# A fused attention and feed-forward block on one core: the first batch taken tile by tile, and the last product split into three pieces

## The chip, the core and the metric

The kernel runs on one core of a Trainium2 chip. The core has five engines that work side by side, each with its own queue of instructions taken in order: PE (TensorE, matrix products into PSUM), DVE (VectorE), ACT (ScalarE), POOL (GpSimd) and SP (SyncE, which here only issues DMA transfers). They wait for each other through semaphores. The metric is the time of one launch in device microseconds (us). Times are of one core, so the slowest core is this one.

## What is computed

Eight batches of 1024 rows with 256 columns, all in float32. Each row is normalized (`xn`), goes through an attention without softmax and through a feed-forward layer, and both results are added to the row:

```python
xn = layernorm(x)                                  # x: (8, 1024, 256)
qkv = xn @ qkv_w + qkv_b                           # 16 heads of 16 columns
q, k = l2norm(q), l2norm(k)
kv = einsum('bhnd,bhne->bhde', k, v)
attn = einsum('bhnd,bhde->bhne', q, kv) @ proj_w + proj_b
ffn = relu(xn @ W1 + b1) @ W2 + b2                 # 256 -> 1024 -> 256
out = x + attn + ffn
```

## The kernel before

**Tiling.** A batch is eight tiles of 128 rows, numbered 0 to 7. Tiles 0 to 3 are its first half, 4 to 7 its second. Products need the rows as columns, so `xn` is turned into `xnT`. For the first batch this is done on PE (`turn_on_pe`, L279: a turn of a 128x128 block is a PE operation against an identity, four to a PSUM bank, and a 128x512 copy by ACT or DVE takes the bank to `xnT`). For later batches DVE and DMA do it while other work runs. The hidden layer, the later projections and the output product are formed by a seven-product scheme over 2x2 blocks: sums of blocks (`sums_of_x`, `sums_of_w1`, `s3_of_x` and their like, on POOL) replace the eighth product.

**Order.** The schedule is manual: each engine runs its instructions in the order in which the program text issues them. An instruction that has to wait holds up everything behind it on its own engine. PSUM tiles named by `bank` (L90) rotate through seven buffers, so a new one waits until the tile seven places back has been read.

**The start.** `load` (L96) issues the loads of `x` on SP: L128 brings the first half of batch 0 in two pieces of two tiles, L129 the query and key weights, L130 the second half in two pieces, L131 the bias of query and key (`qkvb_sb`, spread to all partitions). Then come `b1`, `w1` and the value weights. At L874 PE runs 20 turns of the identity (`WARM`). `norm_stats` (L241) forms mean and variance on DVE and the square root on ACT; `norm_scale` (L255) takes the reciprocal; `norm_apply` (L264) scales a tile on DVE (L275) or on ACT (L271). L877 to L888 do this for tiles 0 to 3, turn them, and then for tiles 4 to 7.

**The projection of batch 0.** `project` (L313) takes tile after tile: two products into one bank (L330, `kc` 0 and 1), the addition of the bias on DVE (L334), the squares on ACT (L336), and their sums on DVE (L339), delayed by one tile. `between` runs a function behind a given tile: `second_half` (L892), behind tile 2, turns tiles 4 to 7 and the rows of `b1` and issues the block sums of x. Behind the projection come L901 to L903 (a block sum, the load of batch 1 into the same `x` buffer, the remaining weights), and then the loop over batches, which begins with `hidden` (L635 is its product).

**The end.** `second` (L764) forms the output product. For the last batch, the second half's output is turned back on PE (`back_on_pe`, L807: turns at L813, addition to `x` at L818) instead of by DVE and POOL. Its last block has two pieces of 256 columns in two banks (`ds`, `parts`, L824 and L825): both products are issued (L860), then both sums on DVE (L862), then for each piece the turn, the addition and a store on SP (L867). The first half's rows go out by four stores (`store(0)`, L803), also on SP.

The lines on which the two ends turn:

```python
load(0, (0,), 2)
load_wqkv(of_qk)
load(0, (1,), 2)
load_qkvb(of_qk)
```

Of the kernel before, what the change touches and what calls it, by code (L numbers as in the profile page):

```python
# [9 lines left out]
F32 = mybir.dt.float32  # L10
AF = mybir.ActivationFunctionType
# [5 lines left out]
def kernel(  # L17
# [46 lines left out]
    S = 32  # L64
    R = P // S
    NP, HP = NT // 2, HT // 2
    WARM = 20
    LN_EPS = 1e-5
    L2_EPS = 1e-12

# [10 lines left out]
    def rows_v(v, b, n):  # L81

        return v[b].rearrange("(n p t) c -> n p t c", n=2, p=P)[n]
# [6 lines left out]
    def bank(shape, name):  # L90

        return psum.tile(shape, F32, tag="bank", name=name)

    xs, xqs, xns, xnTs, xSs, hTs, qks, qTs, mixes, Ms, hSs = ({} for _ in range(11))

    def load(b, halves=(0, 1), pieces=1):  # L96

        if b not in xs:
            xs[b] = one.tile([P, NT, C], F32, tag="x", name=f"x_{b}")
        gt = HT // pieces  # L100
        for n in halves:
            for g in range(pieces):
                nc.sync.dma_start(
                    out=xs[b][:, n * HT + g * gt : n * HT + (g + 1) * gt, :],
                    in_=rows_v(x, b, n)[:, ts(g, gt), :],
                )

    def load_squares(b, halves=(0, 1)):
        xqs[b] = one.tile([P, 2, R, HT, CJ], F32, tag="xq", name=f"xq_{b}")
# [15 lines left out]
        nc.sync.dma_start(out=qkvb_sb[:, cols], in_=qkv_b[cols].partition_broadcast(P))  # L125

    of_qk, of_v = slice(0, 2 * C), slice(2 * C, 3 * C)
    load(0, (0,), 2)  # L128
    load_wqkv(of_qk)  # L129
    load(0, (1,), 2)  # L130
    load_qkvb(of_qk)  # L131
    b1_rows = one.tile([FC, P], F32, tag="gT", name="b1_rows")
    nc.sync.dma_start(out=b1_rows, in_=b1.rearrange("(k p) -> k p", p=P))
# [107 lines left out]
    def norm_stats(b, tiles):  # L241

        xt, n = xs[b], len(tiles)
        st = work.tile([P, NT, 6], F32, tag="st", name=f"st_{b}_{tiles[0]}")[:, :n, :]
        mv = small.tile([P, NT, 2], F32, tag="mv", name=f"mv_{b}_{tiles[0]}")[:, :n, :]
        for i, t in enumerate(tiles):
            nc.vector.bn_stats(st[:, i, :], xt[:, t, :])
        for i in range(n):
            nc.vector.bn_aggr(mv[:, i, :], st[:, i, :])
        rstd = small.tile([P, NT], F32, tag="rstd", name=f"rstd_{b}_{tiles[0]}")[:, :n]  # L250
        nc.scalar.activation(rstd, mv[:, :, 1], AF.Sqrt, bias=eps_sb)
        for i, t in enumerate(tiles):
            stats[b, t] = i, mv, rstd

    def norm_scale(b, tiles, on_act):  # L255
        i, mv, rstd = stats[b, tiles[0]]
        nc.vector.reciprocal(rstd, rstd)
        if on_act:
            nmr = small.tile([P, NT], F32, tag="nmr", name=f"nmr_{b}_{i}")[:, : len(tiles)]
            nc.vector.scalar_tensor_tensor(nmr, mv[:, :, 0], -1.0, rstd, ALU.mult, ALU.mult)  # L260
            for t in tiles:
                stats[b, t] += (nmr,)

    def norm_apply(b, tiles):  # L264
        if b not in xns:
            xns[b] = one.tile([P, NT, C], F32, tag="xn", name=f"xn_{b}")
        for t in tiles:
            xt, xn = xs[b][:, t, :], xns[b][:, t, :]
            i, mv, rstd, *nmr = stats.pop((b, t))
            if nmr:  # L270
                nc.scalar.activation(  # L271
                    xn, xt, AF.Identity, bias=nmr[0][:, i : i + 1], scale=rstd[:, i : i + 1]
                )
            else:
                nc.vector.tensor_scalar(  # L275
                    xn, xt, mv[:, i, 0:1], rstd[:, i : i + 1], ALU.subtract, ALU.mult
                )
# [32 lines left out]
            turns["x", b] = turn(xnTs[b], xns[b], f"x_{b}")  # L310
        next(turns["x", b])

    def project(b, between={}, with_norms=True):  # L313


        xnT = xnTs[b]
        if b not in qks:
            qks[b] = one.tile([P, NT, 2 * C], F32, tag="qk", name=f"qk_{b}")
        qk = qks[b]
        late = []  # L320
        for h in range(2):
            ss = small.tile([P, HT, 2 * H], F32, tag="ssk" if h else "ssq", name=f"ss_{b}_{h}", bufs=1)
            all_ss[b, h] = ss
            for s in range(2):
                norms_of[b, h, s] = ss[:, :, ts(s, H)]
            for i in range(HT):
                t = h * HT + i
                pq = bank([P, 512], f"pq_{b}_{t}")
                for kc in range(KC):
                    nc.tensor.matmul(  # L330
                        pq, xnT[:, kc, t // 2, :, t % 2], wqkv_sb[:, kc, 0 : 2 * C],
                        start=(kc == 0), stop=(kc == KC - 1),
                    )
                nc.vector.tensor_tensor(qk[:, t, :], pq, qkvb_sb[:, 0 : 2 * C], ALU.add)  # L334
                sq = work.tile([P, 2 * C], F32, tag="yt", name=f"sq_{b}_{t}")
                nc.scalar.activation(sq, qk[:, t, :], AF.Square)  # L336
                while late:
                    late.pop(0)()
                late.append(lambda ss=ss, sq=sq, i=i: nc.vector.tensor_reduce(  # L339
                    ss[:, i, :], sq.rearrange("p (g d) -> p g d", d=D), AX.X, ALU.add  # L340
                ))
                if i == HT - 1 and with_norms:
                    late.append(lambda h=h, ss=ss: norms(b, h, ss))
                between.get(t, lambda: None)()
        while late:
            late.pop(0)()

# [408 lines left out]
    def product(dst, lhs, rhs, start, stop):  # L756

        for n, (l, r) in enumerate(zip(lhs, rhs)):
            nc.tensor.matmul(  # L759
                dst, l, r, start=start and n == 0, stop=stop and n == len(lhs) - 1,  # L760
                skip_group_check=True,
            )

    def second(b, early=lambda: None, between=lambda: None):  # L764
# [17 lines left out]
        def add(dst, p, q):  # L782
            nc.vector.tensor_tensor(dst, p, q, ALU.add)
            return dst
# [19 lines left out]
            for j in range(R):  # L804
                nc.sync.dma_start(out=squares_v(out, b, n, j), in_=xq[ts(j, S), n])

        def back_on_pe(m, y, us, name):  # L807


            tp = bank([P, HP, 2, R, S], f"tp{name}_{b}")  # L810
            for u in us:
                for w in range(2):
                    nc.tensor.transpose(  # L813
                        tp[:, u, w].rearrange("p j c -> p (j c)"), y[:, u, :, w], ident
                    )
            xh = xs[b].rearrange("p (n u w) (j m c) -> n m p (u w) j c", n=2, w=2, m=2, c=S)[1, m]
            at = slice(2 * us[0], 2 * us[-1] + 2)
            nc.vector.tensor_tensor(  # L818
                xh[:, at], xh[:, at], tp.rearrange("p u w j c -> p (u w) j c")[:, at], ALU.add
            )  # L820

        a, c_, d, e = (bank([P, HP, P, 2], f"po{s}_{b}") for s in "acde")

        ds = [d] if b < B - 1 else [d[:, 0], bank([P, HP, P, 2], f"pof_{b}")[:, 1]]  # L824
        parts = [slice(0, HP)] if b < B - 1 else range(HP)  # L825
        product(a, b11, a11, True, False)
        u1 = tmp("u1")
        nc.scalar.copy(u1, a)
# [1 line left out]
        u2 = add(tmp("u2"), c_, u1)  # L830
        early()
        u3 = tmp("u3")
        for du, u in zip(ds, parts):
            product(du, t3, [r[:, u] for r in s3], True, False)
            add(u3[:, u], du, u2[:, u])
        between()

        product(e, t1, s1, True, False)
# [13 lines left out]
        if b < B - 1:  # L852
            product(d, t4, a22, False, True)
            join(1, 0, d, u2)
            store(1)
        else:
            back_on_pe(1, y22, range(HP), "o22")
            y21 = tmp("y")
            for u in range(HP):
                product(ds[u], t4, [r[:, u] for r in a22], False, True)  # L860
            for u in range(HP):
                nc.vector.scalar_tensor_tensor(  # L862
                    y21[:, u], ds[u], ob[:, 2, 0:1], u2[:, u], ALU.add, ALU.add
                )
            for u in range(HP):
                back_on_pe(0, y21, (u,), f"o21_{u}")
                nc.sync.dma_start(  # L867
                    out=rows_v(out, b, 1)[:, ts(u, 2), :],
                    in_=xs[b][:, HT + 2 * u : HT + 2 * u + 2, :],
                )  # L870
        yield


    warm = bank([P, HT, P], "warm")  # L874
    for i in range(WARM):
        nc.tensor.transpose(warm[:, i % HT, :], ident, ident)
    norm_stats(0, range(0, 2))  # L877
    norm_stats(0, range(2, 4))
    xnTs[0] = big.tile([P, KC, NP, P, 2], F32, tag="xnT", name="xnT_0")
    for g in (0, 2):  # L880
        norm_scale(0, range(g, g + 2), False)
        norm_apply(0, range(g, g + 2))
    turn_on_pe(xnTs[0], xns[0], "x_0", (0,), (nc.scalar.copy, nc.vector.tensor_copy))
    for g in (4, 6):
        norm_stats(0, range(g, g + 2))
    for g in (4, 6):
        norm_scale(0, range(g, g + 2), True)
        norm_apply(0, range(g, g + 2))  # L888
    sums_of_w1()
    b1_sb = const.tile([P, FC], F32, tag="b1", name="b1_sb")  # L890

    def second_half():  # L892
        turn_on_pe(xnTs[0], xns[0], "x_0", (1,))
        b1_ps = bank([P, FC], "b1_ps")
        nc.tensor.transpose(b1_ps, b1_rows, ident[:FC, :FC])
        nc.vector.tensor_copy(b1_sb, b1_ps)
        sums_of_x(0, 0)
        sums_of_x(0, 1)

    project(0, {HT - 2: second_half}, False)  # L900
    s3_of_x(0)  # L901
    load(1)
    load_rest()  # L903
# [79 lines left out]
```

## Time and profile before

The median of three runs is 619.12 us (618.82 to 619.12). The profiled execution took 620.73 us, of which the span that the trace covers is 619.0 us.

| | busy us | share of the span |
|---|---|---|
| PE | 609.8 | 99% |
| POOL | 421.0 | 68% |
| DVE | 409.6 | 66% |
| PE weight loads | 346.1 | 56% |
| ACT | 210.1 | 34% |

| moment | us from the start of the span |
|---|---|
| first turn of the identity on PE | 1.36 |
| first tile pair of `x` landed, statistics begin | 3.46 |
| first turn of `xn` on PE | 6.27 |
| first product of the projection | 8.47 |
| first product of the hidden layer | 24.90 |
| last addition on DVE | 613.98 |
| end of the span | 619.0 |

The program has 6600 instructions and moves 43.3 MB by DMA, a mean of 70 GB/s. The mean granted clock of PE is 0.994 of full speed.

Reading: "busy" is the time in which an engine had an instruction running. A granted clock of 1.00 is PE's full speed. A row of the timeline gives the start, the duration, the engine, the line, the operation with what it writes and reads, the count, and in brackets how long the engine had been idle and what released it. The "chain that ended last" follows the program back from its last instruction, at each step to what released it.

### The profile page before, as it was taken

To read this page: it belongs to the slowest core of one execution; us is meant where nothing else is said; L and a number is where in the kernel's file an instruction comes from. 1 tells how busy PE (TensorE), PEld (TensorE's weight loads), DVE (VectorE), ACT (ScalarE), POOL (GpSimd) and SP (SyncE) were. 2 spreads that over 40 slices of the span, in tenths; PEclk is the share of its full clock that TensorE was granted. 3 is DMA by queue.
4 is the path that set the end of the run, shared out by engine and by line. 5 is a ranking of instruction groups with operands and counts; after the bars stand their busy time and mean duration, and the time that the engine had idled before them with its cause. 6 is when DMAs were issued, how large, how long until landed. Compare 5 with 4: busy or idle time off the path is not lost.

```text
span 619.0 us, 6600 instructions
## 1 busy us (share of the span) xinstructions
PE 609.8 (99%) x2011; PEld 346.1 (56%) x2011; DVE 409.6 (66%) x733; ACT 210.1 (34%) x355; POOL 421.0 (68%) x346
## 2 busy tenths in 40 slices
PE   8999999999999999999999999999999999999996
PEld 5465446457554666447564484644846457654454
DVE  5777754778748767577756876567865678527823
ACT  4355404352133513244142432425224352103500
POOL 2477997499916997279954799339992599914701
PEclk8999999999999999999999999999999999999998
DMA  7633101580026700275004820058101550004202
GB/s 237 131 66 97 40 0 31 123 176 13 0 52 141 147 2 1 71 167 103 0 1 111 172 58 1 15 123 172 33 0 35 128 110 1 0 7 97 69 1 68
DMA packets 139508, 43.32 MB, mean 70 GB/s; under 512 B 135880, under 2 KB 136272, under 8 KB 139472
## 3 DMA queue, kind: packets, MB, share of 16 engines
q1 hardware_dynamic: 139472, 42.89, 31.2%
q8 instruction: 16, 0.26, 0.2%
q14 instruction: 20, 0.16, 0.1%
HBM read 19.80 MB, written 8.39 MB: 46 GB/s over the span
## 4 chain that ended last, share of the span: by engine, by line
PE 96%; DVE 2%; DMA 1%; issue 0%; ACT 0%; SPq 0%; DVEq 0%; ACTq 0%
PE poa L759 11%; PE poe L759 11%; PE pod L759 10%; PE pha L635 8%; PE phe L635 8%; PE phd L635 8%; PE poc L759 6%; PE pq L330 5%; PE phc L635 4%; PE pqa L398 3%; PE pqe L398 3%; PE pqd L398 3%; PE gpe L565 2%; PE gpd L565 2%; PE gpa L565 2%; PE pqc L398 2%
## 5 line engine op out<-in xcount | busy, mean ns | idle before, releaser
L796 POOL TENSOR_TENSOR xq<-xq,yt_o 128x512 f32<-128x512 f32 x30 | 37.9, 1265 | 122.6 <-DVE yt_o L791 122.6
L642 ACT ACTIVATE hT<-hT,b_sb 128x512 f32<-128x512 f32 x96 | 68.9, 722 | 63.2 <-DVE hT L647 58.4
L190 POOL TENSOR_TENSOR hS<-hT 128x512 f32<-128x512 f32 x31 | 46.5, 1499 | 40.2 <-ACT hT L642 40.2
L635 PE MATMUL pha<-xnT,w_sb 128*128 128x512 f32 x128 | 65.4, 592 | 0.0
L759 PE MATMUL poa<-hT,w_sb 128*128 128x512 f32 x128 | 57.6, 592 | 0.0
L376 ACT ACTIVATE sq<-qk 128x512 f32<-128x512 f32 x48 | 28.9, 626 | 71.1 <-DVE qk L404 59.1
L647 DVE TENSOR_TENSOR hT<-phe,u 128x512 f32<-128x512 f32 x64 | 43.7, 684 | 6.7 <-PE phe L635 4.8
L192 POOL TENSOR_TENSOR hS<-hT,hS 128x512 f32<-128x512 f32 x31 | 39.6, 1276 | 2.4
L191 POOL TENSOR_TENSOR hS<-hS,hT 128x512 f32<-128x512 f32 x31 | 39.5, 1273 | 2.4
L791 DVE STREAM_TRANSPOSE yt_o<-y_o 128x512 f32<-128x512 f32 x30 | 33.0, 1099 | 11.4 <-ACT y_o L847 9.1
L194 POOL TENSOR_TENSOR hT<-hT 128x512 f32<-128x512 f32 x31 | 40.0, 1291 | 0.0
L759 PEld LDWEIGHTS poa<-hT,w_sb 128*128 128x128 f32 x128 | 23.8, 190 | 24.7 <-issue 24.2
L635 PEld LDWEIGHTS pha<-xnT,w_sb 128*128 128x128 f32 x128 | 23.8, 190 | 23.4 <-issue 22.2
L661 ACT COPY u<-pha 128x512 f32<-128x512 f32 x32 | 18.4, 575 | 51.6 <-PE pha L635 51.6
L647 DVE TENSOR_TENSOR u<-phc,u 128x512 f32<-128x512 f32 x32 | 21.8, 682 | 19.7 <-ACT u L661 10.6
L642 ACT ACTIVATE hT<-pha,b_sb 128x512 f32<-128x512 f32 x32 | 21.9, 683 | 33.2 <-PE pha L635 33.2
L635 PE MATMUL phe<-xS,w1t 128*128 128x512 f32 x64 | 32.7, 592 | 0.0
L635 PE MATMUL phe<-xS,w_sb 128*128 128x512 f32 x64 | 32.7, 592 | 0.0
L635 PE MATMUL phc<-xS,w1t 128*128 128x512 f32 x64 | 32.7, 592 | 0.0
L635 PE MATMUL phd<-xnT,w1t 128*128 128x512 f32 x64 | 32.7, 592 | 0.0
L635 PE MATMUL phd<-xnT,w_sb 128*128 128x512 f32 x64 | 32.7, 592 | 0.0
L271 ACT ACTIVATE xn<-x,nmr,rstd 128x256 f32<-128x256 f32 x56 | 28.4, 587 | 6.6 <-PE gpd L565 4.1
(191 smaller groups left out, 1311.5 us busy)
## 6 DMA issues: line engine op xcount, KB each, us to landing
xq<-in_L_attn_x_dram SPq DMA_DIRECT2D x60, 128.0 KB, 3.7
out_dram<-xq SPq DMA_DIRECT2D x60, 128.0 KB, 2.8
x<-in_L_attn_x_dram SPq DMA_DIRECT2D x14, 512.0 KB, 6.4
xnT<-turn_x SPq DMA_DIRECT2D x112, 64.0 KB, 2.1
qT<-turn_q SPq DMA_DIRECT2D x112, 64.0 KB, 2.2
x<-in_L_attn_x_dram SPq DMA_DIRECT2D x4, 256.0 KB, 4.0
w_sb<-in_L_ffn_W_dram SPq DMA_DIRECT2D x2, 512.0 KB, 7.8
w_sb<-in_L_ffn_W_dram SPq DMA_DIRECT2D x8, 128.0 KB, 3.2
```

The lines of the kernel that those rows point to most:

```text
L190: eng.tensor_tensor(s1, a21, a22, ALU.add)
L191: eng.tensor_tensor(s2, s1, a11, ALU.subtract)
L192: eng.tensor_tensor(s4, a12, s2, ALU.subtract)
L194: eng.tensor_tensor(a21, a11, a21, ALU.subtract)
L398: nc.tensor.matmul(dst[:, w, :], a[:, g, :, w], rhs, start=start and w == 0, stop=stop, skip_group_check=True,)
L565: nc.tensor.matmul(dst, l[:, t, :], r[:, t, :], start=start and t == 0, stop=stop and t == HT - 1, skip_group_check=True,)
L635: nc.tensor.matmul(dst, lhsT, rhs, start=start, stop=stop, skip_group_check=True)
L642: nc.scalar.activation(block(i, n, m), src, AF.Relu, bias=b1_sb[:, fc : fc + 1])
L647: nc.vector.tensor_tensor(dst, p, q, ALU.add)
L759: nc.tensor.matmul(dst, l, r, start=start and n == 0, stop=stop and n == len(lhs) - 1, skip_group_check=True,)
L791: nc.vector.transpose(yt.rearrange("p u w r c -> p u r w c"), y.rearrange("p u (s r) w -> p u r w s", r=R),)
L796: nc.gpsimd.tensor_tensor(xh, xh, yt.rearrange("p u w r c -> p (u w) r c"), ALU.add)
```

## The change

Start: 16 turns of the identity instead of 20. Tiles 0 and 1 are loaded singly, then the weights of query and key, then tiles 2 and 3, 4 and 5, 6 and 7 as pairs. Tiles 0 and 1 are each normalized by themselves, scaled on DVE and turned by a new `turn_tile`: two turns into one bank and one 128x256 copy on ACT. Tiles 2 and 3 are normalized before the projection begins and turned inside it, between the two products of tile 1. The same function then normalizes tiles 4 to 7 (4 and 5 scaled on ACT, 6 and 7 on DVE). These are turned between the two products of tile 3. The squares of tiles 0 to 2 are held until tile 3 has been projected.

End: the last batch's last block has three pieces, of 256, 128 and 128 columns, in three banks. The sum of a piece stands directly behind its product, and its turn behind the product of the next piece. Three stores instead of two: tiles 0 and 1 and then tile 2 of the second half are issued by ACT, tile 3 by SP.

```diff
-    WARM = 20
+    WARM = 16
...
-    load(0, (0,), 2)
+    load(0, (0, 1, 2))
     load_wqkv(of_qk)
-    load(0, (1,), 2)
+    load(0, (2, 4, 6, 8))
     load_qkvb(of_qk)
...
-    def project(b, between={}, with_norms=True):
+    def project(b, within={}, held_to=0, with_norms=True):
...
                 for kc in range(KC):
                     nc.tensor.matmul(
                         pq, xnT[:, kc, t // 2, :, t % 2], wqkv_sb[:, kc, 0 : 2 * C],
-                        start=(kc == 0), stop=(kc == KC - 1),
+                        start=(kc == 0), stop=(kc == KC - 1), skip_group_check=True,
                     )
+                    if kc == 0:
+                        within.get(t, lambda: None)()
                 nc.vector.tensor_tensor(qk[:, t, :], pq, qkvb_sb[:, 0 : 2 * C], ALU.add)
...
+                def square(t=t, ss=ss, i=i):
+                    sq = work.tile([P, 2 * C], F32, tag="yt", name=f"sq_{b}_{t}")
+                    nc.scalar.activation(sq, qk[:, t, :], AF.Square)
+                    return lambda: nc.vector.tensor_reduce(
+                        ss[:, i, :], sq.rearrange("p (g d) -> p g d", d=D), AX.X, ALU.add
+                    )
+
+                held.append(square)
+                while held and t >= held_to:
+                    late.append(held.pop(0)())
+                    while len(late) > 1:
+                        late.pop(0)()
...
-        def back_on_pe(m, y, us, name):
+        def back_on_pe(m, y, tiles, name):
...
-        ds = [d] if b < B - 1 else [d[:, 0], bank([P, HP, P, 2], f"pof_{b}")[:, 1]]
-        parts = [slice(0, HP)] if b < B - 1 else range(HP)
+        if b < B - 1:
+            parts = [lambda r: r]
+        else:
+            parts = [lambda r: r[:, 0], lambda r: r[:, 1, :, 0], lambda r: r[:, 1, :, 1]]
+        ds = [parts[0](d)] + [
+            part(bank([P, HP, P, 2], f"po{s}_{b}")) for s, part in zip("fg", parts[1:])
+        ]
...
+            for k in range(len(ds) + 1):
+                if k < len(ds):
+                    part = parts[k]
+                    product(ds[k], t4, [part(r) for r in a22], False, True)
+                    nc.vector.scalar_tensor_tensor(
+                        part(y21), ds[k], ob[:, 2, 0:1], part(u2), ALU.add, ALU.add
+                    )
+                if k == 1:
+                    back_on_pe(0, y21, (0, 1), "o21_0")
+                    last_store(nc.scalar, 0, 2)
+                elif k > 1:
+                    back_on_pe(0, y21, (k,), f"o21_{k}")
+                    last_store(nc.scalar if k == 2 else nc.sync, k, 1)
...
+    def turn_tile(t):
+
+        tp = bank([P, KC, P], f"tpx_{t}")
+        for kc in range(KC):
+            nc.tensor.transpose(tp[:, kc, :], xns[0][:, t, ts(kc, P)], ident)
+        nc.scalar.copy(xnTs[0][:, :, t // 2, :, t % 2], tp)
+
+    for t in range(2):
+        norm_stats(0, (t,))
+    for t in range(2):
+        norm_scale(0, (t,), False)
+        norm_apply(0, (t,))
+        turn_tile(t)
+    norm_stats(0, (2, 3))
+    norm_scale(0, (2, 3), True)
+    norm_apply(0, (2, 3))
     sums_of_w1()
...
-    def second_half():
-        turn_on_pe(xnTs[0], xns[0], "x_0", (1,))
+    def tiles_2_3():
+        for t in (2, 3):
+            turn_tile(t)
+        norm_stats(0, (4, 5))
+        norm_stats(0, (6, 7))
+        norm_scale(0, (4, 5), True)
+        norm_scale(0, (6, 7), False)
+        norm_apply(0, (4, 5))
+        norm_apply(0, (6, 7))
+
+    def tiles_4_to_7():
+        for t in range(HT, NT):
+            turn_tile(t)
...
-    project(0, {HT - 2: second_half}, False)
+    project(0, {1: tiles_2_3, 3: tiles_4_to_7}, 3, False)
     s3_of_x(0)
     load(1)
     load_rest()
```

`last_store` issues one DMA on the engine that it is given. The new `back_on_pe` turns and adds single tiles instead of pairs. The same pieces are used for the earlier of the two products into these banks: for the last batch it too runs in three pieces.

More of the change, by code (lines that the diff above doesn't have):

```diff
@@ L94, with load @@
     xs, xqs, xns, xnTs, xSs, hTs, qks, qTs, mixes, Ms, hSs = ({} for _ in range(11))
-    def load(b, halves=(0, 1), pieces=1):
+    def load(b, cuts=(0, HT, NT)):
         if b not in xs:
             xs[b] = one.tile([P, NT, C], F32, tag="x", name=f"x_{b}")
[L100 to L106, printed above, removed]
+        for i, j in zip(cuts, cuts[1:]):
+            n = i // HT
+            nc.sync.dma_start(
+                out=xs[b][:, i:j, :], in_=rows_v(x, b, n)[:, i - n * HT : j - n * HT, :]
+            )
     def load_squares(b, halves=(0, 1)):
@@ L319, in project @@
         qk = qks[b]
-        late = []
+        late, held = [], []
         for h in range(2):
@@ L331, in project @@
                         pq, xnT[:, kc, t // 2, :, t % 2], wqkv_sb[:, kc, 0 : 2 * C],
-                        start=(kc == 0), stop=(kc == KC - 1),
+                        start=(kc == 0), stop=(kc == KC - 1), skip_group_check=True,
                     )
+                    if kc == 0:
+                        within.get(t, lambda: None)()
                 nc.vector.tensor_tensor(qk[:, t, :], pq, qkvb_sb[:, 0 : 2 * C], ALU.add)
[L335 to L341, printed above, removed]
+                def square(t=t, ss=ss, i=i):
[9 more added lines that the diff above has]
+                        late.pop(0)()
                 if i == HT - 1 and with_norms:
                     late.append(lambda h=h, ss=ss: norms(b, h, ss))
-                between.get(t, lambda: None)()
         while late:
@@ L805, in store @@
                 nc.sync.dma_start(out=squares_v(out, b, n, j), in_=xq[ts(j, S), n])
-        def back_on_pe(m, y, us, name):
[L810 to L820, printed above, removed]
-        a, c_, d, e = (bank([P, HP, P, 2], f"po{s}_{b}") for s in "acde")
-        ds = [d] if b < B - 1 else [d[:, 0], bank([P, HP, P, 2], f"pof_{b}")[:, 1]]
-        parts = [slice(0, HP)] if b < B - 1 else range(HP)
+        def back_on_pe(m, y, tiles, name):
+            tp = bank([P, HT, R, S], f"tp{name}_{b}")
+            for t in tiles:
+                nc.tensor.transpose(
+                    tp[:, t].rearrange("p j c -> p (j c)"), y[:, t // 2, :, t % 2], ident
+                )
+            xh = xs[b].rearrange("p (n t) (j m c) -> n m p t j c", n=2, m=2, c=S)[1, m]
+            at = slice(tiles[0], tiles[-1] + 1)
+            nc.vector.tensor_tensor(xh[:, at], xh[:, at], tp[:, at], ALU.add)
+        a, c_, d, e = (bank([P, HP, P, 2], f"po{s}_{b}") for s in "acde")
+        if b < B - 1:
[5 more added lines that the diff above has]
+        ]
         product(a, b11, a11, True, False)
@@ L832, in second @@
         u3 = tmp("u3")
-        for du, u in zip(ds, parts):
-            product(du, t3, [r[:, u] for r in s3], True, False)
-            add(u3[:, u], du, u2[:, u])
+        for du, part in zip(ds, parts):
+            product(du, t3, [part(r) for r in s3], True, False)
+            add(part(u3), du, part(u2))
         between()
@@ L856, in second, with last_store @@
         else:
-            back_on_pe(1, y22, range(HP), "o22")
+            back_on_pe(1, y22, range(HT), "o22")
             y21 = tmp("y")
[L859 to L863, printed above, removed]
-                )
[L865 to L870, printed above, removed]
+            def last_store(eng, t, n):
+                eng.dma_start(
+                    out=rows_v(out, b, 1)[:, t : t + n, :], in_=xs[b][:, HT + t : HT + t + n, :]
+                )
+            for k in range(len(ds) + 1):
[4 more added lines that the diff above has]
+                        part(y21), ds[k], ob[:, 2, 0:1], part(u2), ALU.add, ALU.add
+                    )
+                if k == 1:
[4 more added lines that the diff above has]
+                    last_store(nc.scalar if k == 2 else nc.sync, k, 1)
         yield
@@ L876 @@
         nc.tensor.transpose(warm[:, i % HT, :], ident, ident)
-    norm_stats(0, range(0, 2))
-    norm_stats(0, range(2, 4))
     xnTs[0] = big.tile([P, KC, NP, P, 2], F32, tag="xnT", name="xnT_0")
[L880 to L888, printed above, removed]
+    def turn_tile(t):
[12 more added lines that the diff above has]
+    norm_apply(0, (2, 3))
     sums_of_w1()
     b1_sb = const.tile([P, FC], F32, tag="b1", name="b1_sb")
-    def second_half():
-        turn_on_pe(xnTs[0], xns[0], "x_0", (1,))
+    def tiles_2_3():
[10 more added lines that the diff above has]
+            turn_tile(t)
         b1_ps = bank([P, FC], "b1_ps")
```

## The prediction

> **What bounds the kernel now.** I read the page first (busy shares and the chain that ended last), then TensorE's waits, then the timeline of the first 25 us and of the last 12 us, since the diff touches only these two ends.
>
> ```profile
> PE 609.8 (99%) x2011; PEld 346.1 (56%) x2011; DVE 409.6 (66%) x733; ACT 210.1 (34%) x355; POOL 421.0 (68%) x346
> ...
> PE 96%; DVE 2%; DMA 1%; issue 0%; ACT 0%; SPq 0%; DVEq 0%; ACTq 0%
> ```
>
> TensorE is busy 99% of the span and is 96% of the chain. Between the ends it idles once, 0.7 us before `of_rows`. So whatever starts TensorE's steady stream earlier arrives at the end almost whole, and whatever shortens the time after its last matmul counts fully. The head, from the timeline (start, duration, engine, line):
>
> ```profile
> 6.27 0.65 PE L285 MATMUL tpx<-ident,xn 128*128 128x128 f32 x2 [1.03 <-DVE xn L275]
> ...
> 8.47 6.78 PE L330 MATMUL pq<-wqkv_sb,xnT 128*128 128x512 f32 x12
> ...
> 11.85 0.69 DVE L334 TENSOR_TENSOR qk<-pq,qkvb_sb 128x512 f32<-128x512 f32 x1 [0.24 <-PE pq L330]
> ...
> 24.90 1.02 PE L635 MATMUL pha<-xnT,w_sb 128*128 128x512 f32 x2
> ```
>
> The projection starts at 8.47, when four tiles are normalized, turned and copied, and the hidden layer starts at 24.90. One projection product is two records of 0.43 us (0.86), so 16 products need 13.8 us; they take longer because the clock was halved at first. I cut the head at the steps of the granted clock (columns: stretch, length, busy time of PE, PEld, DVE, ACT, POOL, then granted clock, DMA share, GB/s):
>
> ```profile
> 4.41:7.82 3.41, 2.18 (x13) 1.39 (x13) 2.59 (x11) 0.61 (x3) 0.00 (x0) 1.00 0.98 293
> 7.82:11.24 3.42, 3.38 (x8) 1.42 (x7) 2.63 (x11) 1.21 (x4) 0.00 (x0) 0.50 0.97 332
> ```
>
> After a stretch in which PE was busy 2.18 of 3.41 us (64%), the next 3.42 us ran at 0.50. From 8.47 that is 2.77 us at half speed, 1.39 us lost. DMA is full throughout, which matters for one load:
>
> ```profile
> qkvb_sb<-in_L_attn_qkv_b_dram SPq DMA_DIRECT2D x1, 256.0 KB, 6.9
> ```
>
> It is issued at 3.54, so the bias lands at 10.44. Nobody waits for it now, since its first reader, the addition at 11.85, is released by PE.
>
> The tail (the chain's last pieces, then the store queue):
>
> ```profile
> 612.48 0.49 DVE y_o L862
> 612.98 0.04 issue
> 613.02 0.52 PE tpo L813 x2
> 613.54 0.02 issue
> 613.56 0.42 DVE x L818
> ```
> ```profile
> 611.04 2.63 SPq L805 DMA_DIRECT2D out_dram<-xq  x4
> 613.76 1.24 SPq L867 DMA_DIRECT2D out_dram<-x  x2
> ```
>
> Compute ends at 613.98. Six stores leave one queue at about 0.6 us each, and the last, issued at 614.4, lands 3.5 us later at 617.9. Another 1.1 us closes the program at 619.0.
>
> **The change, part by part: the head.** Loads: tile 0 alone (128 KB) instead of a pair that landed at 3.44. The nearest rows are that one and a 0.2 KB load, which takes 2.0 us (2.74), so I take 3.1. Tiles 2 and 3 move behind the two weight loads, whose places in the byte order move up, so they land at about 6.45 (where the second weight load landed, issued 2.1 plus 4.35) instead of 4.67.
>
> Tile 0 then costs: statistics 0.41, aggregate 0.17, Sqrt 0.29 on ACT, then behind tile 1's statistics the reciprocal 0.14 and the scaling 0.41, ready at 4.79. Two transposes take 0.44 to their result. The 128x256 copy on ACT has no row: between 0.266 (128x128) and 0.61 (128x512), by columns 0.38. The first projection product starts at 5.74 instead of 8.47. The four fewer warm-up transposes cost nothing, as PE would wait for tile 0 anyway; their 16 still run past 4.41.
>
> Now the order that follows. Tiles 2 and 3 (from 6.45: statistics 1.0, Sqrt and two small operations 0.65, ACT scaling 0.59 each) can be turned at 8.79 and 9.31. PE has finished product 3 at 8.32 and loses 0.8 us. It then runs products 4 to 7 (the half of tile 1, tile 2, the first half of tile 3) to 12.96.
>
> Here the change adds a wait. On DVE the bias addition of tile 0 now stands **ahead** of the statistics of tiles 4 to 7; before, these stood ahead of all additions. Its PE result is there at 7.7, but the bias is not. The same 1.5 MB go ahead of it in one more issue, so I keep 10.46. Behind it on DVE, by the pitches of the trace:
>
> - addition of tile 0: 0.65, to 11.1
> - statistics and aggregates of 4 and 5: 0.67 + 0.30, to 12.1, and of 6 and 7 to 13.05
> - reciprocal and bias factor: 0.32, to 13.37. ACT scales 4 and 5 to 13.98 and 14.5, and PE turns them
> - reciprocal and two scalings of 6 and 7: 0.88, to 14.25
> - addition of tile 1: 0.7, to 14.95. It also waits in this queue, and the turn of tile 6 needs the PSUM bank that it frees (seven rotate)
>
> PE turns 6 and 7 and the b1 rows in 0.54, to 15.5. Then come the second half of tile 3 (0.86) and tiles 4 to 7 (eight products, 6.88): the hidden layer starts at 15.5 + 0.86 + 6.88 = **23.24** instead of 24.90, a gain of **1.66**. This chain hangs on the bias alone: the early start at 5.74 is spent in waiting, about 2.4 us of PE in all. Were the bias there by 8.1, ACT's queue (copies of 2 and 3 to 10.15, then Sqrt and scaling to 12.0) would keep up with PE, and the hidden layer would start at about 21.7.
>
> The held squares cost no PE time: four on ACT (0.63) and four reductions on DVE (0.68) are worked off beside tiles 4 to 7, where DVE needs 1.37 per tile against PE's 1.72. By my sum DVE is level again at tile 7, 0.4 us to spare. If it were not, the wait before `of_rows` would grow by as much, since DVE leads the chain there. The `x` load for the next batch waits for the last reader of tile 5, 14.5 instead of 13.27, and with it 28 SP issues behind it (to about 36.5 instead of 35.3). The next reader is the statistics at 31.96, and SP's next transposing stores come at 48.4, so nothing. POOL's sums of x start behind its weight sums at 17.0 instead of 17.80.
>
> **The tail.** The second piece becomes two of 128 columns: ten records each at 0.111 (the row of the 128-column products of `mix_g`), 1.11 each, so 2.22 for 2.17. The earlier product into these banks (L834) is cut likewise, another 0.05 on PE; its one more addition on DVE lies beside the eight products of `poe`. The new banks wait for nothing: each was read over 2 us before. Their operands and banks are read and written with a stride of two. The nearest row is the turn of `y_o`, whose strided operand runs at the usual 0.11, so I add nothing; the upper end is a doubled 2.2 us, and a gain is excluded since the work is the same. PE ends its products at 612.56. DVE: the last piece's 128x128 sum (between 0.29 for a 128x128 addition and 0.48 for 128x256, so 0.35) from 612.78, tile 2's addition 0.29, the turn of tile 3 0.33 beside it, its addition to 613.83 (was 613.98). Stores: ACT, idle since 604, issues tiles 0 and 1 at 612.2 (was 613.76) and tile 2 at 613.4; SP has finished its four at 613.67 and issues tile 3 at 613.87 (last issue was 614.4). No row shows an issue on ACT; I take SP's 0.57 to 0.64, with 0.43 (SP's loads) and twice that as ends.
>
> How much arrives? The engines' busy shares from 612.2 to 617.2 sum to 3.86 us of full work. 0.85 of it is done by 613.6, when ACT's first bytes can move (0.8 us behind the issue, as with SP's first store). At a share of 0.95 the rest ends at 616.8 instead of 617.2. The tail gains **0.45**, between 0 (single-tile rows of 1 KB move worse) and 0.9.
>
> **Rule against row: the clock.** The Trainium skill, "TensorE: Matmul & The Clock Gate", section "Why this matters for your kernels", asks only that PE have no idle gap above about 3 us. By that the new gaps (none above 1.1 us) cost nothing, but neither should the old ones (1.03 and 0.20) have halved the clock at 7.82. So the row decides: 64% busy lost it, and a later stretch with 79% (34.0 to 37.4, PE 2.69 of 3.40) kept it. In the new order 4.41 to 7.82 is filled nearly wholly (kept; the half-speed stretch of before goes), but 11.24 to 14.65 holds the bias wait: 1.88 of products, 0.53 of turns, **71%**. By the rule it keeps the clock (gain 1.66 stays); by the row it may lose it at 14.65, and half speed from about 15.0 to 18.06 costs 1.53. I take it as kept, being nearer in kind to the 79% case (most of it full products, where the 64% were short transposes), and hold the other as a rival.
>
> **Sum.** 1.66 + 0.45 - 0.05 = 2.1 us. The profiled execution would go from 620.73 (span 619.0 plus 1.73 around it) to about 618.6. The median of the runs, 619.12, lies 1.6 below that execution; I subtract the same: **617.0**. A measurement of this kernel can tell 0.2% (1.24 us) from no change.
>
> **Rivals.**
> - *The starved stretch loses the clock* (618.5): 1.66 - 1.53 + 0.45 = 0.6 gained. For it: 71% is nearer to 64 than one would like. Against: its matmuls are dense.
> - *The bias is early, or nothing waits for it* (615.5): head 3.2, tail 0.45. For it: fewer bytes are ahead if the queue's order is kept loosely. Against: 6.9 us to landing with DMA at 0.97.
> - *Slower: the clock gained by before in timed runs, lost by after* (619.9). The profiled run is 1.61 above the median; if that is the cold 1.39, timed runs have no cold stretch to win back. Head 1.66 - 1.39 - 1.53 = -1.26, tail +0.45: 0.8 slower. It decides where both waits of PE (1.1 before 14.0, 0.5 after) fall into one stretch of the clock, and from a bias that lands 0.45 later it is over 0.2%.
>
> **Chances.** Forecast 0.50 (its own range 616.2 to 617.9), lost clock 0.20, early bias 0.12, slower 0.18. Range 615.4 to 619.2: it takes in all but the slower case and the outermost part of the early one. Faster by over 0.2%: nearly all of the forecast, the early bias, a fifth of the lost clock: 0.64. Slower by over 0.2%: two thirds of the slower case: 0.13. Rest 0.23.
>
> **What would show it.** First `pq` near 5.7; the first bias addition released by the DMA near 10.5; a PE gap from 13 to 14 and another before the turn of tile 6; first `pha` near 23.2; granted clock 1.00 from 4.4 on; DVE's last addition near 613.8 less 1.7, last landing 3.6 us after it. Wrong if the first addition waits for PE, if the clock falls at 14.7, or if strided pieces take over 1.3 us each.

## The result, and the profile after

The changed kernel is slower: 620.40 us median of nine runs (619.92 to 622.37) against 619.01 us of nine runs before (618.82 to 619.16). The ratio of the mean times is 1.003, with a 95% interval of 1.0019 to 1.0042. Forecast was 617.0, with a range of 615.4 to 619.2. The profiled executions of both kernels (620.73 before, 622.37 after) are longer than their medians: each holds a stretch of TensorE at half clock, and its mean granted clock (0.994 and 0.995) is lower than that of most executions of its kernel.

The page of the changed kernel (busy shares, then the chain) looks as before, so the loss is not in the body:

```profile
PE 611.1 (98%) x2027; PEld 346.5 (56%) x2027; DVE 411.6 (66%) x736; ACT 211.8 (34%) x361; POOL 421.1 (68%) x346
...
PE 95%; DVE 2%; DMA 1%; SPq 0%; issue 0%; ACT 0%; DVEq 0%; ACTq 0%
```

The timeline of its head answers row by row to the one of before:

```profile
6.11 3.21 PE L328 MATMUL pq<-wqkv_sb,xnT 128*128 128x512 f32 x6
...
11.06 0.69 DVE L334 TENSOR_TENSOR qk<-pq,qkvb_sb 128x512 f32<-128x512 f32 x1 [2.61 <-DMA qkvb_sb<-in_L_attn_qkv_b_dram]
...
13.73 1.27 POOL L184 TENSOR_TENSOR w1t<-w_sb,w1t 128x512 f32<-128x512 f32 x1
...
14.11 2.32 DVE L273 TENSOR_SCALAR xn<-x,mv,rstd 128x256 f32<-128x256 f32 x2
14.42 1.28 PE L897 MATMUL tpx<-ident,xn 128*128 128x128 f32 x6 [0.91 <-ACT xn L269]
...
16.57 0.41 PE L897 MATMUL tpx<-ident,xn 128*128 128x128 f32 x2 [0.87 <-DVE xn L273]
...
26.71 1.02 PE L640 MATMUL pha<-xnT,w_sb 128*128 128x512 f32 x2
```

The projection does start at 6.11 instead of 8.47. Then DVE idles 2.61 us for the bias, and everything behind that addition is late. The two scalings of tiles 6 and 7 take 2.32 us, with GpSimd's weight sums beside them. PE waits 0.91 us for tile 4 and 0.87 us for tile 7 (the six turns at 14.42 are those of tiles 4, 5 and 6). The hidden layer starts at 26.71. Last, the clock (columns as in the prediction, cut at the steps of this trace's clock):

```profile
13.72:17.13 3.41, 1.69 (x9) 0.85 (x9) 3.20 (x6) 2.39 (x7) 3.40 (x3) 1.00 0.01 3
17.13:20.54 3.41, 3.41 (x5) 1.63 (x6) 1.73 (x4) 1.32 (x3) 3.25 (x4) 0.50 0.89 310
```

PE was busy 50% of the first stretch, and the next ran at half speed.

At the end (store queues; ACTq is ACT's), the stores of the last block start earlier than the old ones, moved by the 1.81 us that the hidden layer is late, would have (613.98 against 615.57). But the issues of SP's four first-half stores take 3.35 us instead of 2.63, and that of its last store 1.04 instead of about 0.6:

```profile
612.85 3.35 SPq L810 DMA_DIRECT2D out_dram<-xq  x4
...
613.98 1.58 ACTq L868 DMA_DIRECT2D out_dram<-x  x2
...
616.29 1.04 SPq L868 DMA_DIRECT2D out_dram<-x  x1
```

### The profile page after: what moved, and what is told of

Its sections match the earlier page's. It is cut to its first block, busy times and chain, and to the rows that moved or that the text cites. A ratio compares the mean times of both kernels' runs of the same rounds, so it can differ in the third digit from the quotient of the medians.

```text
span 620.6 us, 6646 instructions
## 1 busy us (share of the span) xinstructions
PE 611.1 (98%) x2027; PEld 346.5 (56%) x2027; DVE 411.6 (66%) x736; ACT 211.8 (34%) x361; POOL 421.1 (68%) x346
## 4 chain that ended last, share of the span: by engine, by line
PE 95%; DVE 2%; DMA 1%; SPq 0%; issue 0%; ACT 0%; DVEq 0%; ACTq 0%
PE poa L764 11%; PE poe L764 11%; PE pod L764 10%; PE pha L640 8%; PE phe L640 8%; PE phd L640 8%; PE poc L764 6%; PE phc L640 4%; PE pq L328 4%; PE pqe L403 3%; PE pqa L403 3%; PE pqd L403 3%; PE gpe L570 2%; PE gpd L570 2%; PE gpa L570 2%; PE pqc L403 2%
```

## The experiments

Ten kernels ran, each in five rounds beside the kernel before, whose medians there were 619.02, 619.03 and 618.94.

| run | median us | ratio to before (95%) | first hidden product in its profile |
|---|---|---|---|
| e1_head | 621.37 | 1.0035 (1.0022 to 1.0047) | 24.86 |
| e2_tail | 619.15 | 1.0004 (0.9996 to 1.0013) | 23.09 |
| e3_add_late | 618.14 | 0.9982 (0.9975 to 0.9989) | 22.30 |
| e4_67_on_act | 620.51 | 1.0027 (1.0016 to 1.0038) | 24.55 |
| e5_pool_later | 619.33 | 1.0004 (0.9996 to 1.0012) | 22.69 |
| e6_fill | 620.77 | 1.0025 (1.0014 to 1.0036) | 25.57 |
| e7_bias_early | 621.64 | 1.0047 (1.0034 to 1.0059) | 25.72 |
| e8_tail_sp | 619.06 | 1.0005 (0.9998 to 1.0011) | 23.17 |
| e9_x23_first | 617.89 | 0.9979 (0.9969 to 0.9990) | 21.92 |
| e10_late_old_end | 617.91 | 0.9983 (0.9976 to 0.9990) | 22.47 |

In all twelve profiles, of these ten and the two kernels, the time of the profiled execution less the moment of its first hidden product lies between 595.66 and 596.13. So what differs between them is made at the start. The three with the old end have 595.67 to 595.83, the nine with the new end 595.66 to 596.13.

**Which end loses?** e1_head has the new start and the old end; e2_tail the reverse.

> The new start with the old end. Theory (the whole loss is made at the start: TensorE is starved between 13.2 and 17.3 us and then runs a stretch at half clock, while the end gains about 0.2): about 620.6, 1.4 to 1.8 slower than before, first hidden product near 26.7 in a profile that shows the half clock and near 25 in one that doesn't. Rival (the start gains its 1.7 as forecast in runs without a profile's own clock, and the end with its two store queues loses 3): about 617.3.

> The old start with the new end. Theory: 0.2 to 0.4 faster than before, about 618.7, with four first-half stores that take longer to issue than before (0.8 instead of 0.66 each) and the last store landing about 5 us after DVE's last addition less 1.4. Rival: about 3 slower, 622.

The head loses all of it. The end comes out at no difference that can be told, not the 0.2 to 0.4 gain expected. e1's median is above the expected 620.6: three of its five runs have a mean granted clock of 0.995 (621.37 to 622.41), and the other two (0.998 and 0.997) took 620.58 and 621.09. That spread is too wide to say that the new end helped the changed kernel.

The profile of e2_tail also shows what the old start usually costs. Its first hidden product:

```profile
23.09 1.02 PE L635 MATMUL pha<-xnT,w_sb 128*128 128x512 f32 x2
```

That is 1.8 us earlier than the 24.90 of the profile that the prediction read, and no stretch at half clock follows its turns. Of the 1.8, 0.46 is there at the first product of the projection (8.01 instead of 8.47), and the rest is the half clock behind it. The two executions differ in when the clock first goes to full speed, 4.42 in the profile of before and 6.26 in e2_tail: in the first the 20 turns of the identity were over at 5.23 and PE was idle until 6.27, in the second the slower turns filled the time until 5.89. e8_tail_sp, with the same start, has 23.17.

**Is it what stands behind the bias addition?**

```diff
-                nc.vector.tensor_tensor(qk[:, t, :], pq, qkvb_sb[:, 0 : 2 * C], ALU.add)
+                adds.append(lambda t=t, pq=pq: nc.vector.tensor_tensor(
+                    qk[:, t, :], pq, qkvb_sb[:, 0 : 2 * C], ALU.add
+                ))
+                while adds and (t > 0 or not within):
+                    adds.pop(0)()
```

> The changed kernel, but the bias addition of tile 0 is issued behind the statistics and scaling of tiles 4 to 7 instead of ahead of them. The same work. Theory (what stands behind the late bias in VectorE's queue starves TensorE): statistics of 4 to 7 from about 8.5 to 11.5, scaling of 6 and 7 over before GpSimd starts at 12.4 and so 0.4 each instead of 1.2, first hidden product near 22.2, granted clock full from 4.4 on; 617.2 (3.2 faster than the changed kernel's 620.4). Rival (the bias wait is harmless, TensorE waits for the tiles' loads or for PSUM banks): the first hidden product stays above 24.5 and the time above 619.5.

It is. The same instructions, with one addition moved behind eleven small ones and two scalings on DVE, make the changed kernel 2.3 us faster and faster than before. Rows of e3_add_late:

```profile
11.17 0.74 DVE L273 TENSOR_SCALAR xn<-x,mv,rstd 128x256 f32<-128x256 f32 x2
11.82 1.88 DVE L334 TENSOR_TENSOR qk<-pq,qkvb_sb 128x512 f32<-128x512 f32 x3
...
22.30 1.02 PE L644 MATMUL pha<-xnT,w_sb 128*128 128x512 f32 x2
```

The scalings are over before GpSimd starts at 12.14 and take 0.74. The addition now finds the bias landed. The first hidden product is where it was expected (22.2), but the time gained is 2.3, not 3.2. The start that this is to be compared with is one with the full clock (24.86 in e1_head), and from there the gain is 2.6.

**How much is GpSimd?** e4_67_on_act moves the scaling of 6 and 7 to ACT; e5_pool_later keeps it on DVE and makes GpSimd wait for it.

```diff
-        norm_scale(0, (6, 7), False)
+        norm_scale(0, (6, 7), True)
```

> The changed kernel, but tiles 6 and 7 are scaled by ScalarE as 4 and 5 are, the bias wait left as it is. Theory (two causes add up, the bias wait and VectorE's scaling being held up by GpSimd's sums, 2.32 us for two operations instead of 0.75): the turn of tile 6 at about 15.5 instead of 16.57, the second half of tile 3 at 16.3 instead of 17.3, 1.0 faster than the changed kernel and up to 1.7 more where the clock then stays full: 618.0 to 619.4. Rival A (the bias wait is all, the slow scaling lies beside it): no change, 620.4. Rival B (the slow scaling is all): 617.5 or less.

```diff
     norm_apply(0, (2, 3))
-    sums_of_w1()
+    token = const.tile([P, 1], F32, tag="token", name="token")
...
         norm_apply(0, (6, 7))
+        nc.gpsimd.tensor_copy(token, xns[0][:, 7, 0:1])
+        sums_of_w1()
```

> The changed kernel, but GpSimd's sums of the hidden weights wait for tile 7 to be scaled (one more small GpSimd copy that reads that tile), so that no GpSimd operation runs beside VectorE's two scalings. The bias wait is left. Theory (with GpSimd out of the way the two scalings take 0.75 instead of 2.3 us, and the turn of tile 6 hangs on them): scaling 14.1 to 14.9, turn of tile 6 near 15.6 instead of 16.6, first hidden product near 23.9, 619.4, 1.0 faster than the changed kernel. Rival (the scaling of 6 and 7 takes as long for another reason, or ScalarE's two tiles are as late anyway): 620.4.

By the time alone e4 looks like its rival A (no change), but it is not a clean test: four scalings in ACT's queue end about as late as the two held-up ones on DVE (16.14 against 16.43). e5 is the clean one, and its time came out as forecast, 619.33 against 619.4. Its rows:

```profile
10.05 0.69 DVE L334 TENSOR_TENSOR qk<-pq,qkvb_sb 128x512 f32<-128x512 f32 x1 [1.74 <-DMA qkvb_sb<-in_L_attn_qkv_b_dram]
...
13.10 0.74 DVE L273 TENSOR_SCALAR xn<-x,mv,rstd 128x256 f32<-128x256 f32 x2
...
22.69 1.02 PE L640 MATMUL pha<-xnT,w_sb 128*128 128x512 f32 x2
```

With GpSimd out of the way the scalings take 0.74 again. In this execution the bias came early (10.05; that is why the first hidden product is at 22.69 and not near the expected 23.9), so the distance from the bias addition to the first hidden product is the fair measure: 12.64 here. It is 14.02 in e1_head and 13.96 in e6_fill, where GpSimd interferes and the clock stays full, and 15.65 in the changed kernel's profile, which has both costs. So in the profiles GpSimd costs about 1.4 and the half clock, where it occurs, about 1.65. By the medians, the 2.3 us between the changed kernel and e3 divide into 1.1 for GpSimd (620.40 to 619.33) and 1.2 for the bias wait that e5 still has (619.33 to 618.14).

**The clock.** e6_fill puts turns of the identity into PE's two waits:

```diff
+        fill = ps_mix.tile([P, HT, P], F32, tag="mix", name="fill")
         for t in range(HT, NT):
+            for i in range({HT: 9, HT + 2: 12}.get(t, 0)):
+                nc.tensor.transpose(fill[:, i % HT, :], ident, ident)
             turn_tile(t)
```

> The changed kernel with 21 more turns of the identity in TensorE's two waits before the turns of tile 4 and of tile 6; they fit into the waits. Theory (the long runs of the changed kernel, 621.9 to 622.4 in a third of its runs, are those in which a starved stretch costs the clock): these runs disappear, none above 621.2, the median 620.2. Rival A (the clock falls by its own phase): a third of the runs stay at about 622. Rival B (the lost clock is in all runs and makes the whole loss): median 618.7.

None of its seven runs is above 621.6, where three of the changed kernel's nine are between 621.87 and 622.37; their mean granted clock is 0.995 to 0.996, that of the other six 0.997 to 0.999. All seven have 0.997 to 0.999. The limit of 621.2 was missed, and the median is no better. The rows of the starved stretch in e6_fill and, without the fill, in e1_head, each cut at the steps of its own clock:

```profile
11.70:15.11 3.41, 2.56 (x14) 1.57 (x13) 3.16 (x13) 1.28 (x4) 2.19 (x2) 1.00 0.40 145
15.11:18.52 3.41, 3.35 (x23) 2.64 (x23) 3.04 (x5) 2.15 (x6) 3.21 (x4) 1.00 0.17 28
```
```profile
12.68:16.09 3.41, 2.27 (x9) 0.80 (x7) 3.16 (x9) 2.49 (x7) 3.33 (x4) 1.00 0.04 13
16.09:19.50 3.41, 3.04 (x9) 1.62 (x10) 2.70 (x7) 1.43 (x3) 3.33 (x3) 1.00 0.66 226
```

With the fill the worst stretch is 75% busy (2.56 of 3.41), and the next one keeps 1.00. But e1_head kept it with 67%, so a starved start does not always cost the clock. Seven runs are few (if a third of them lost the clock, none in seven would still happen about 6 times in 100), so that starvation causes the long runs is likely rather than shown. That the clock is not the cause of the median's loss is shown: the six runs of the changed kernel with 0.997 or more took 619.92 to 620.61, and the profiled executions of e1_head, e4_67_on_act and e6_fill, whose traces keep full speed through the start, took 620.58, 620.59 and 621.60. Nor is every long run a lost clock: the kernel before had runs of 620.30 and 620.44 at 0.999 and 1.0, and nothing here explains them.

**Can the bias come earlier instead?**

```diff
-    load(0, (2, 4, 6, 8))
     load_qkvb(of_qk)
+    load(0, (2, 4, 6, 8))
```

> The changed kernel, but the bias is loaded directly behind the weights of query and key, ahead of tiles 2 to 7; VectorE's order is left. Theory (the bias's late landing at 11.0 is what starves TensorE): the bias lands near 8.2, the first addition waits for nothing after that, tiles 2 and 3 land about 0.9 later (near 7.6), scaling of 6 and 7 is over before GpSimd starts; first hidden product near 23.1, 618.4. Rival (the bias's transfer is slow by itself, about 7 us wherever it stands in the queue, and holds up what follows): it lands at 9.5 or later, tiles 4 to 7 too, and the time stays above 619.8.

The rival is nearer: 621.64, no better than the changed kernel (three of the five runs have a mean granted clock of 0.994 to 0.996; the other two took 620.98 and 621.23). The bias lands 5.3 us after its issue instead of 6.9 and is waited for by nobody, as the theory had it, but the tiles behind it pay for it. Rows of e7_bias_early, from the timeline:

```profile
8.90 0.75 DVE L245 BATCH_NORM_STATS2 st<-x 128x6 f32<-128x256 f32 x2 [3.28 <-DMA x<-in_L_attn_x_dram]
...
11.28 1.18 PE L897 MATMUL tpx<-ident,xn 128*128 128x128 f32 x4 [2.36 <-ACT xn L269]
```

Tiles 2 and 3 land at 8.90 instead of about 6.7, so PE waits 2.36 us before the turn of tile 2. The next stretch of the clock (11.00 to 14.41) ran at 0.50, and the scalings of 6 and 7 stood beside GpSimd again, 2.52 us for the two, so the time does not measure the delay alone. The bias is 256 KB and costs what is behind it 2.1 us, about 120 GB/s.

**The second store queue.** e8_tail_sp issues all three last stores on SP.

> The old start with the new end, but all three last stores on SyncE's queue. Theory (the two queues hold each other up in issuing: SyncE's fourth store took 1.36 us and its last 1.06 instead of 0.6): all of SyncE's issues take about 0.6 again, the first-half stores land after 2.9 instead of 4.4, the last issue ends at about the same time as with two queues, and the time is 619.0 to 619.3, so the second queue brought nothing. Rival (the second queue gains as forecast and something else in the new end loses it): 619.5 or more.

Its store rows:

```profile
609.48 2.63 SPq L805 DMA_DIRECT2D out_dram<-xq  x4
612.21 1.84 SPq L863 DMA_DIRECT2D out_dram<-x  x3
```

One queue issues all seven by 614.05, at 0.6 each; two queues (e2_tail, an execution whose end runs 0.25 earlier) end at 613.74 with SP's issues stretched to as much as 1.36. The first-half stores land 2.9 us after issue here and 4.4 with two queues. The times are the same.

**What is left to gain.** e9_x23_first is e3_add_late with tiles 2 and 3 loaded ahead of the weights; e10_late_old_end is e3_add_late with the old end.

```diff
-    load(0, (0, 1, 2))
+    load(0, (0, 1, 2, 4))
     load_wqkv(of_qk)
-    load(0, (2, 4, 6, 8))
+    load(0, (4, 6, 8))
```

> The bias addition of tile 0 issued late (as in the run of that name), and tiles 2 and 3 loaded ahead of the weights of query and key again. Theory (with the bias wait gone the next limit is that tiles 2 and 3 land at 6.75 and are turned at 9.1, when TensorE has been free since 8.65): tiles 2 and 3 land near 5.0, weights near 6.4, first projection product near 6.2, no wait before the turn of tile 2, first hidden product near 21.7, 617.6. Rival (the weights land later and take it back): first hidden product at 22.3 or later, 618.1 or more.

> The new start with the late bias addition, and the old end (two pieces, all stores on SyncE). Theory (the new end is worth nothing): 618.1 as with the new end, within 0.2. Rival (the forecast's 0.45 for the end holds once the start is in order): 618.6.

Both come near to their theory. e9 has the earliest first hidden product, 21.92, and both are faster than either kernel, by 1.0 to 1.1 us against before; e9 and e10 themselves cannot be told apart. The old end with the late addition is as good as the new end (617.91 against 618.14 in e3), so that end gains nothing that can be told.

## Why the prediction was wrong

- **Right in mechanism.** The early start of the projection (5.74 forecast, 6.11 measured), the bias addition released by the DMA, its place ahead of the statistics as the thing that starves PE, the wait of PE before tile 4 and a second one (forecast before tile 6, measured before tile 7), and the chain from the bias to the hidden layer: 12.78 us in the sum (10.46 to 23.24), 12.64 in the run without GpSimd's interference.
- **First failed term: "reciprocal and two scalings of 6 and 7: 0.88, to 14.25".** They took 2.5 (13.91 to 16.43), and the chain became 1.4 longer. The pitch was read from scalings that ran alone (two in 0.73 at 5.80). The trace of before also had scalings beside GpSimd's sums, four in 2.42:

```profile
42.86 2.42 DVE L275 TENSOR_SCALAR xn<-x,mv,rstd 128x256 f32<-128x256 f32 x4 [3.17 <-PE gp L502]
43.16 1.32 POOL L194 TENSOR_TENSOR hT<-hT 128x512 f32<-128x512 f32 x1
```

The new order puts the two beside the sums of the weights from 12.4 on. The rows of the changed kernel, one by one:

```profile
14.11 1.04 DVE L273 TENSOR_SCALAR xn<-x,mv,rstd 128x256 f32<-128x256 f32 x1
14.96 1.32 POOL L184 TENSOR_TENSOR w_sb<-w_sb 128x512 f32<-128x512 f32 x1
15.07 1.36 DVE L273 TENSOR_SCALAR xn<-x,mv,rstd 128x256 f32<-128x256 f32 x1
```

Each scaling ends 0.15 us behind the GpSimd addition that ran when it began (15.15 behind 15.00, 16.43 behind 16.28). The Trainium skill states the rule in "SBUF — State Buffer", section "Who interferes with whom": VectorE's two-port operations, of which a scaling can be one, and GpSimd's operations take a shared pair of ports for a whole instruction, and the second one blocks. The trace agrees in the times: 1.16 us each beside GpSimd, 0.37 without. That it is the ports, no run here shows.
- **Second: "The same 1.5 MB go ahead of it in one more issue, so I keep 10.46".** The additions that waited for the bias began at 10.05, 10.84, 11.06, 11.08 and 11.61 in five profiles, a mean of 10.93: half a microsecond later than one landing in another order had suggested.
- **Third, and as large: "I subtract the same".** The forecast counted winning back a cold stretch of 1.39 us that the profiled execution had and the median runs did not. With the old start at about 23.1 instead of 24.90, a hidden layer at 23.24 would have gained nothing to begin with. The prediction named this in its slower rival (619.9, 0.18), which is what happened, though with GpSimd's 1.4 in place of the lost clock.
- **The end, 0.45, measured 0.** "I take SP's 0.57 to 0.64" was wrong on both sides: ACT issued in 0.34 to 0.37, and with two queues SP's own issues grew to 1.36 and 1.06 (e2_tail). Why they grew stays open: the one of 1.06 began at 612.68, when ACT's last issue had been over for 0.74 us. Compute ended no earlier: DVE's last addition is over at 615.76, and the old end's 613.98, moved by the 1.81 us that the hidden layer starts later, gives 615.79.
- **The clock, rule against row.** The row was the better guide. Each trace records when the clock first goes to full speed (4.17 to 6.89 us from the start of the span), and its later steps lie on multiples of 3.41 us from there. Cut at the steps of their own trace, stretches that were 39% (e7_bias_early), 50% (changed kernel) and 64% busy (before) were followed by half speed. Stretches of 66% (e4_67_on_act), 67% (e1_head), 75% (e6_fill) and 79% (e10_late_old_end) were not. No gap in them reached 3 us, so the rule was too weak. The forecast's 71% lies on the side that kept the clock; measured was 50%. Part of it is luck: e1_head, with the same start, has its waits divided between two stretches (67% and 89%), because its first step came at 5.85 and not at 6.89. (The prediction's own 79% was not cut at the steps: at them it is 82% and 98%.) The lost clock costs a third of the runs, not the median.

Together: 0.1 lost on the head by a better reference (23.1 to 23.24), about 0.5 by the bias and 1.4 by GpSimd is 2.0 slower; 1.4 was measured. The other 0.6 is not accounted for. The terms are read from single profiled executions, in which the bias landed anywhere from 10.05 to 11.61; by the medians GpSimd's term is 1.1.

## What to carry to other kernels

Before an instruction that waits for a late load is placed, ask what stands behind it on its engine: moving one addition behind work that was ready turned 1.4 us lost into 0.9 gained. An operation's duration belongs to its neighbours too, so take it from a row with the same engines busy beside it. When the profiled execution is longer than the median, find out where before forecasting against the median, above all if the change touches that place.

## What the hardware showed unexpectedly

- A DMA issue on SP took 0.6 us with one store queue and up to 1.36 us with ACT's as a second one.
- Spreading a bias to all partitions (256 KB) delayed the loads behind it by 2.1 us.
- Whether a starved start cost the clock depended on where the steps of the clock fell in that execution: 50% busy in one stretch of 3.41 us lost it, 67% and 89% in two did not.
- A scaling on DVE of about 0.4 us took up to 1.36 us beside GpSimd's additions of 1.3 us, and ended just behind them.
